# Mixed inputs made transposed by TensorE at once, with the residual turned back by VectorE

## The chip, the cores and the metric

The kernel runs on one core of a Trainium2 chip. The metric is device time in microseconds (us) for one execution; lower is better. All arithmetic is in fp32.

The engines are named as in the profile: PE is TensorE's matmuls and PEld its weight loads, DVE is VectorE, ACT is ScalarE, POOL is GpSimd, SP is SyncE, which here only issues DMAs.

## The reference

There are 64 batches of 32 tokens with 512 features. Two layers with residuals follow each other:

```python
x = x + einsum('bct,bcd->bdt', x, W[cond])     # per batch one of 16 matrices, 32x32, mixes the 32 tokens
q, k, v = x @ Wq.T, x @ Wk.T, x @ Wv.T         # 32 query heads, 8 key/value heads, 128 wide
q, k = rope(rmsnorm(q)), rope(rmsnorm(k))
kc, vc = k_cache[block_table], v_cache[block_table]      # 512 cached tokens for each batch, masked by length
probs = softmax(mask(q @ concat(kc, k).T * SCALE))
x = x + (probs @ concat(vc, v)) @ Wo.T
```

The first line is what the change is about. Its result is called x1 below. It is needed twice: transposed (features on the partitions), as the stationary or moving side of the projections, and in rows, as the residual of the second layer.

## The kernel before

**Tiling.** Four batches make a tile of 128 rows (tokens); there are NT = 16 tiles. The 8 key/value heads are worked on in two halves (hh = 0 and 1) of 4. So there are 32 steps, n = hh * 16 + t, each with one tile and one half of the heads. A step has 4 batches x 4 slots = 16 slots of about 4 us each. The inputs x1 are made in the first half alone; the second half reads what was kept in DRAM.

**What sets the order.** SP and PE run in the order in which the program issues; for the opening (all before the slots of step 0) that goes for every engine, elsewhere a scheduler places the rest. Each piece of work that isn't attention is put into a slot by `at(n, slot, ...)`; within a slot it comes in the order of these calls. A store that a piece puts into `kept` is issued on SP KEEP = 2 slots later.

**x1 of a tile, step by step.**
- `x1_a` (L383 on) loads 128 rows of x into `st.acc`. `load_cond_weights` (L288) loads the four batches' 32x32 matrices onto the diagonal of a zeroed 128x128 buffer `bds[t % 2]`, called bd; two such buffers take turns.
- `x1_c` (L404) is one matmul, with bd as weights and the 512 columns of `st.acc` moving, into PSUM (L408); DVE adds the result to `st.acc` (L409), which then holds x1 in rows.
- `x1_b` (L411) makes four 128x128 transposes of `st.acc` on PE with the identity `ident` (L416) into PSUM, and ACT copies them to `st.x1t` (L421).
- `keep_x1t` (L426) and `keep_x1` (L429) store both to DRAM: x1t_d for the second half's projections, acc_d for the residual. `reload` (L974) brings the residual back, when the step's output is to be added to it.

**What uses it.** Steps 0 to 3 are projected one by one (L470, up to `classic`). From step 4 on, two tiles make a `Pair`, whose projections use Strassen's products (in Winograd's form) of 2x2 blocks: `sums_x` (L669 to L673) makes sums of the inputs' blocks on DVE, t2, t3 and t4 (L726 to L733) sums of the weights' blocks, and seven products, "1" to "7", run on PE (L698, in PSUM tiles pa, pb, pc). The pair's x1t lie in one buffer, `early`, with room for seven blocks: two of the first tile, two of the second, and three of sums. The fourth sum, L673, has no room of its own and is written over a block of the second tile's x1t; so it waits until the store of that x1t (L426) has read it. Product 6 uses t2, which stands behind L673 on DVE.

In the first half, a pair's inputs are made in the last slots of the step before the pair's products (`input_of`): mix of the first tile in slot 11, of the second in 12, turned in 13 and 14. For the first pair that has these (n = 4) all is later: 14, 14, 15, 15. For the pair before that (n = 2) they are in slots 4 to 7 of step 2 itself.

**Beside it.** In every slot four score matmuls (L1027, 128x128 weights and 128 columns moving), the exponential on ACT (L1038) and the value matmuls (L1090) run; nv_x (L1101) are DVE's sums of the values. The keys come over SP, a half of a batch at a time in eight DMAs of 64 KB (k_t, L321), and DVE copies them to the buffers kh_x (L1018). Cached values come by indirect DMAs on POOL (L354) and are scaled by ACT (L366). Query and key rows go through L540 (a 32x32-block transposition on DVE), the DRAM buffer heads_d (L544, POOL) and SP (q_ring, L553) to their columns; in the opening and the first steps they go through PE (L527) and a copy (L612).

**The opening.** Tile 0's x1 is made while the projections' weights are still being loaded; `keep_warm` are matmuls whose results are not used. Tile 1's mix and transposes stand between attention work of tile 0.

The kernel can also run an exact version of the attention (`exact`), after a test of the denominators; with these inputs it isn't entered.

Of the kernel before, what the change touches and what calls it, by code (L numbers as in the profile page):

```python
# [12 lines left out]
F32 = mybir.dt.float32  # L13
# [47 lines left out]
def cond_resid_paged_attention_kernel(  # L61
# [118 lines left out]
    def other_half(by):  # L180
# [2 lines left out]

    x1t_d = [
        dram.tile([P, KC * P], F32, tag=f"x1t_d{t}", name=f"x1t_d{t}") for t in range(NT)
    ]
    acc_d = [dram.tile([P, HID], F32, tag=f"acc_d{t}", name=f"acc_d{t}") for t in range(NT)]
    rot_d = {
# [14 lines left out]
    def steps_of(exact, pools):  # L203
# [200 lines left out]
        def x1_c(st):  # L404
            if st.hh:
                return
            pm = ps_p.tile([P, 512], F32, tag="pp", name=f"pmix_{st.name}")
            nc.tensor.matmul(pm, bds[st.t % 2], st.acc, start=True, stop=True)  # L408
            nc.vector.tensor_tensor(st.acc, pm, st.acc, ALU.add)  # L409

        def x1_b(st):  # L411
            if st.hh:
                return
            pm = ps_p.tile([P, KC, P], F32, tag="pp", name=f"px1t_{st.name}")
            for c in range(KC):
                nc.tensor.transpose(pm[:, c, :], st.acc[:, c * P : (c + 1) * P], ident)  # L416
# [4 lines left out]
            nc.scalar.copy(st.x1t, pm)  # L421
            if st.n or exact:
                kept.append(lambda: keep_x1t(st, nc.sync))

        def keep_x1t(st, eng):
            eng.dma_start(x1t_d[st.t], st.x1t.rearrange("p c q -> p (c q)"))  # L426

        def keep_x1(st, eng=nc.sync):
            eng.dma_start(acc_d[st.t], st.acc)  # L429

        trigs = {}

# [538 lines left out]

        def reload(st):
            st.acc = work.tile([P, HID], F32, tag="acc", name=f"res_{st.name}", bufs=2)
            nc.sync.dma_start(st.acc, acc_d[st.t])  # L974

        def new_ot(st):
            st.ot = act.tile([P, QH, P], F32, tag="ot", name=f"ot_{st.name}", bufs=2)
# [273 lines left out]
        number = conditions(0, mybir.EngineType.DVE)  # L1251
        for i in range(BT):
            blk = slice(i * S, (i + 1) * S)
            nc.vector.tensor_copy(
                bds[0][blk, blk], w_all[:, bass.ds(number[i], 1), :].rearrange("p o e -> p (o e)")
            )
        x1_c(first)
        keep_warm(4)
        x1_b(first)
        keep_warm(3)  # L1260
        load_cond_weights(1)
        load_w("q", 0, 3)
        later = Batch(first, 1)
# [39 lines left out]
        for c in (0, 1):  # L1303
            batch.fill(c)
            fetch(1, c)
        v_copy(first, new)
        x1_c(second)
        batch.fill(2)
        fetch(1, 2)
# [2 lines left out]
        values(batch, 0)  # L1312
        q_a(first, 3)
        q_b(first, 2)
        x1_b(second)
        keep_x1(second, nc.gpsimd)
        head_keys(later, 0, nc.scalar)
        head_keys(later, 1, nc.scalar)
        after.load_half()
        rot_tables(second)  # L1320
        k_a(second)
        q_b(first, 3)
        scores(batch, 1)
        scores(batch, 3)
# [33 lines left out]
        def input_of(st, n, load, weights, mix, turned_at):  # L1358
            at(weights[0], weights[1], lambda: load_cond_weights(st.t))
            if load:  # L1360
                at(load[0], load[1], lambda: x1_a(st))
            at(n, mix, lambda: x1_c(st))
            at(n, turned_at, lambda: x1_b(st), lambda: kept.append(lambda: keep_x1(st)))

# [50 lines left out]
        for pair in pairs:  # L1415
            s0, s1 = pair.both
            n = s0.n - 2
            if n == 2:
                input_of(s0, 2, (1, 15), (1, 15), 4, 5)
                input_of(s1, 2, None, (2, 2), 6, 7)  # L1420
                ahead[2, 1].append(lambda st=s1: x1_a(st))
                at(2, 8, lambda: shift_w(0, 0))
                at(2, 9, lambda pair=pair: sums_x(pair))
                angles_of(2, 1, 9, 9)
                tables_of(pair, "q", 2, 8)
                tables_of(pair, "k", 3, 2)
                set_of(pair, 0, 2, {9: "t2", 10: "1", 11: "6 2 t3", 12: "5 t4", 13: "3 7", 14: "4"})
                at(3, 1, lambda: shift_w(0, 1))
                set_of(pair, 1, 3, {2: "t2", 3: "1 6 t3", 4: "2 5 t4", 5: "3", 6: "7", 7: "4"})
                at(3, 6, lambda: shift_w(0, 2))  # L1430
                set_of(
                    pair, 2, 3,
                    {8: "t2 1", 9: "2 t3", 10: "6 t4", 11: "7", 12: "4", 13: "5", 14: "3"},
                )
                spread_of(s0, 3, (12, 12, 13, 13))
            else:
                at(n, 2, lambda pair=pair: sums_x(pair, (0,)))
                at(n, 3, lambda pair=pair: sums_x(pair, (1,)))
                if pair.hh:
                    at(n - 1, 7, lambda st=s0: load_x(st))  # L1440
                    at(n - 1, 10, lambda st=s1: load_x(st))
                    tables_of(pair, "q", n - 1, 6)
                    tables_of(pair, "k", n, 7)
                else:
                    late = int(n == 4)
                    m = (n - 1, 7)
                    input_of(s0, n - 1, m, (n - 1, 6), 11 + 3 * late, 13 + 2 * late)
                    input_of(s1, n - 1, m, (n - 1, 7), 12 + 2 * late, 14 + late)
                    angles_of(s0.n // 2, n - 1, 4, 4 if late else 6)
                    if late:  # L1450
# [99 lines left out]
        for st in steps:  # L1550
            for bt in range(0 if st.n else 1, BT):
# [3 lines left out]
                for g in range(GH):  # L1555
# [27 lines left out]
                    norm_end()  # L1583
                    stores += [(st.n * BT * GH + slot + KEEP, keep) for keep in kept]
                    kept.clear()
                    if slot == 3 and st.n > 1 and st.n - 1 in alone:
                        reload(steps[st.n - 1])
                    if slot == 2 and st.n in twos:
                        reload(twos[st.n].s0)
# [131 lines left out]
```

## Time and profile before

| | |
|---|---|
| median of 3 runs | 2073.85 us (2072.66 to 2074.44) |
| the profiled execution's own time | 2073.99 us |
| its span in the trace | 2072.1 us |
| mean granted clock of TensorE | 0.997 |
| bytes moved by DMA | 413.33 MB, mean 199 GB/s |
| mix L408, a tile, on the chain | 0.86 us |
| four transposes L416, a tile, on the chain | 0.44 us |

How the profile is read: times are in us unless marked ns. A group's row has the line of the program, the engine, the operation, output<-inputs, the shape, and the count. The chain of waits that ended last is followed back from the last instruction, at each step to what released it; as a list in time it has start, duration and what. A timeline row has start, duration, engine, line, operation, and in brackets the idle time before it with what ended it. "x4" is the number of instructions in a row. "q1" in the list of queues is SP's queue: packets, MB, share of 16 DMA engines. "SPq" are DMA issues by SP. A line of waits has the waiting instruction, what ended its waits, us in total, times, longest.

### The profile page before, as it was taken

What the parts mean: (1) busy time and instruction counts of PE and PEld (TensorE: products, weight loads), DVE (VectorE), ACT (ScalarE), POOL (GpSimd) and SP (SyncE); (2) the same over time, 40 slices, a digit from 0 to 9 for tenths busy, and PEclk for the clock granted to TensorE, in tenths of its full rate; (3) what the DMA queues carried; (4) which work ended last, traced back from release to release, by engine and by line L of the source; (5) the groups of instructions that cost most, each with busy time, mean ns of one, the idle gap of its engine ahead of it and who ended that gap; (6) DMA issues with size and microseconds to landing.
All of it is one profiled execution on the core that took longest, in us unless ns stands there. A gap on an engine that the chain in (4) does not pass through costs nothing.

```text
span 2072.1 us, 45314 instructions
## 1 busy us (share of the span) xinstructions
PE 2044.2 (99%) x13460; PEld 1596.7 (77%) x13460; DVE 1629.5 (79%) x3533; ACT 958.4 (46%) x2707; POOL 1002.9 (48%) x1138
## 2 busy tenths in 40 slices
PE   8999999999999999999999999999999999999998
PEld 4767667787887878778786677878878788787897
DVE  4555687988969789697996769879797887979854
ACT  4444354444545444454434445344454445445351
POOL 4354465645636455363544445445363544536351
PEclk9999999999999999999999999999999999999999
DMA  8767557667676666787767876676767667676682
GB/s 244 198 183 223 154 153 233 184 196 217 180 219 191 210 201 189 212 265 223 217 190 208 233 207 195 196 206 180 213 182 216 185 193 210 184 211 180 191 233 75
DMA packets 410144, 413.33 MB, mean 199 GB/s; under 512 B 58944, under 2 KB 325824, under 8 KB 409888
## 3 DMA queue, kind: packets, MB, share of 16 engines
q1 hardware_dynamic: 353472, 228.55, 38.3%
q0 software_dynamic: 55680, 181.58, 28.7%
q8 instruction: 109, 1.79, 0.4%
q14 instruction: 147, 1.20, 0.2%
q10 hardware_dynamic: 736, 0.21, 0.0%
HBM read 350.09 MB, written 60.03 MB: 198 GB/s over the span
## 4 chain that ended last, share of the span: by engine, by line
PE 79%; DVE 7%; DMA 6%; SPq 3%; issue 3%; POOL 2%; ACT 1%; DVEq 0%; POOLq 0%; ACTq 0%
PE ps_x L1027 18%; PE po_x L1090 17%; PE p_x L837 13%; PE pb_x L698 8%; PE pc_x L698 6%; PE pa_x L698 5%; PE pout_x L794 3%; DMA k_t_x<-in_kt_dram 3%; SPq L321 2%; PE pnv_x L1072 2%; PE pp_q_x L470 2%; PE psn_x L1048 1%; DMA raw_x<-in_vc_dram,v_row 1%; PE pp_v_x L470 1%; DVE kh_x L1018 1%
## 5 line engine op out<-in xcount | busy, mean ns | idle before, releaser
L354 POOL DMA_INDIRECT raw_x<-in_vc_dram,v_row x512 | 550.7, 1076 | 626.7 <-ACT v_ring_x L366 513.2
L1038 ACT ACTIVATE pr_x<-ps_x 128x512 f32<-128x512 f32 x511 | 305.4, 598 | 777.5 <-PE ps_x L1027 772.4
L1090 PEld LDWEIGHTS po_x<-v_ring_x,pr_x 128*128 128x128 f32 x4088 | 523.5, 192 | 85.4 <-issue 67.3
L1027 PE MATMUL ps_x<-q_ring_x,kh_x 128*128 128x128 f32 x4088 | 547.7, 277 | 1.6 <-ACT q_ring_x L612 1.6
L1090 PE MATMUL po_x<-v_ring_x,pr_x 128*128 128x129 f32 x4088 | 544.1, 276 | 2.2 <-DVE nv_x L1101 2.2
L1027 PEld LDWEIGHTS ps_x<-q_ring_x,kh_x 128*128 128x128 f32 x4088 | 499.7, 192 | 13.9 <-issue 3.3
L366 ACT ACTIVATE v_ring_x<-raw_x,valid 128x512 f32<-128x512 f32 x512 | 342.9, 713 | 21.9 <-DMA raw_x<-in_vc_dram,v_row 21.5
L1018 DVE COPY kh_x<-k_t_x 128x512 f32<-128x512 f32 x506 | 218.6, 432 | 97.3 <-PE ps_x L1027 68.2
L544 POOL DMA_DIRECT2D heads_d<-rows_x x150 | 125.8, 839 | 278.0 <-DVE rows_x L540 211.1
L698 PE MATMUL pb_x<-t_x,early 128*128 128x512 f32 x504 | 238.4, 596 | 2.6 <-DVE t_x L726 1.2
L1101 DVE TENSOR_TENSOR nv_x<-po_x,nv_x 128x258 f32<-128x258 f32 x256 | 106.8, 417 | 101.3 <-PE po_x L1090 96.6
L837 PEld LDWEIGHTS p_x<-wo_x,ot_x 128*128 128x128 f32 x624 | 116.8, 190 | 62.1 <-issue 45.8
L488 POOL TENSOR_TENSOR rs_q_x<-ms_q_x,minus_half 128x4 f32<-128x4 f32 x128 | 158.7, 1240 | 10.7
L837 PE MATMUL p_x<-wo_x,ot_x 128*128 128x256 f32 x624 | 156.4, 380 | 0.1
L837 PE MATMUL p_x<-ts_x,ot_x 128*128 128x256 f32 x624 | 145.5, 380 | 0.0
L698 PEld LDWEIGHTS pb_x<-t_x,early 128*128 128x128 f32 x504 | 86.2, 191 | 65.4 <-issue 60.6
L837 PEld LDWEIGHTS p_x<-ts_x,ot_x 128*128 128x128 f32 x624 | 115.6, 191 | 24.2 <-issue 8.4
L1104 DVE TENSOR_TENSOR nv_x<-nv_x,rden 128x256 f32<-128x256 f32 x256 | 109.5, 428 | 8.7
L479 ACT ACTIVATE sq_q_x<-u_x 128x128 f32<-128x128 f32 x224 | 66.3, 298 | 93.9 <-DVE u_x L714 93.9
L698 PE MATMUL pc_x<-wq_x,early 128*128 128x512 f32 x224 | 105.4, 593 | 0.0
L698 PE MATMUL pa_x<-wq_x,early 128*128 128x512 f32 x224 | 105.4, 593 | 0.0
L514 DVE TENSOR_TENSOR rope_q_x<-rope_q_x,rs_q_x 128x512 f32<-128x512 f32 x120 | 82.2, 685 | 19.7 <-POOL rs_q_x L488 19.3
(207 smaller groups left out, 2629.6 us busy)
## 6 DMA issues: line engine op xcount, KB each, us to landing
k_t_x<-in_kt_dram SPq DMA_DIRECT2D x2048, 64.0 KB
heads_d<-rows_x POOLq DMA_DIRECT2D x150, 256.0 KB
q_ring_x<-heads_d SPq DMA_DIRECT2D x464, 80.0 KB
raw_x<-in_vc_dram,v_row POOLq DMA_INDIRECT x512
wo_x<-in_wo_dram SPq DMA_DIRECT2D x32, 256.0 KB
res_x<-acc_d SPq DMA_DIRECT2D x31, 256.0 KB
wq_x<-in_wq_dram SPq DMA_DIRECT2D x8, 512.0 KB
early<-x1t_d SPq DMA_DIRECT2D x16, 256.0 KB
```

Source lines behind the costliest of these rows:

```text
L354: nc.gpsimd.indirect_dma_start(out=raw.rearrange("p g d -> p (g d)"), out_offset=None, in_=vc, in_offset=bass.IndirectOffsetOnAxis(ap=v_ro ...
L366: nc.scalar.activation(v_ring[:, c, :, 0:D], raw, AF.Copy, scale=valid[:, b, c : c + 1])
L488: nc.gpsimd.tensor_tensor(rs, ms, minus_half, ALU.pow)
L544: nc.gpsimd.dma_start(heads_d[st.n][:, :, i, :].rearrange("k p c -> p k c"), part)
L698: nc.tensor.matmul(bank, pair.x[:, i, c, :], by[:, c * 512 : (c + 1) * 512], start=start and c == 0, stop=c == 1, skip_group_check=not start,)
L837: nc.tensor.matmul(to, left[:, i, :], right(i), start=start and i == 0, stop=i == QH // 2 - 1, skip_group_check=True,)
L1018: nc.vector.tensor_copy(to, src)
L1027: nc.tensor.matmul(ps[:, c, i, :], ba.k[j][:, i, c, :], queries(ba, g + i), start=True, stop=True,)
L1038: nc.scalar.activation(pr, ps, AF.Exp, scale=SCALE)
L1090: nc.tensor.matmul(ba.po[g][:, i, :], ba.pr[j][:, c, i, :], ba.v_t[:, 2 * half + c, g + i, :], start=(half == 0 and c == 0 and i == 0), st ...
L1101: nc.vector.tensor_tensor(t, ba.po[g], t, ALU.add)
L1104: nc.vector.tensor_tensor(t[:, :, 0:D], t[:, :, 0:D], rd.unsqueeze(2).to_broadcast([P, 2, D]), ALU.mult,)
```

## The change

- `x1_c` no longer mixes rows. The rows of x are the weights, in four chunks of 128 features, and bd moves, with the identity added: out = chunk^T (bd + I), which is x1 of this chunk, transposed. ACT copies it to `st.x1t` in this slot.
- `with_own` adds the identity to bd on DVE, one slot before the mix. For tile 0 it is added in the four copies that build bd.
- `x1_b` no longer uses PE: DVE turns x1t back with its transposition of 32x32 blocks. The blocks then don't lie in rows of 512: partition s of group k holds, for each chunk c and each batch b, 32 features of token s of b.
- `keep_x1` undoes that on the way to DRAM, into a new buffer x1_d: four DMAs for a tile, of 32 partitions x 16 runs of 128 bytes each. `reload` in the first half reads it by four DMAs, one for a batch (32 x 4 runs of 512 bytes).
- Step 0's residual is now reloaded too.
- In the opening, tile 0 is turned back and kept behind `v_copy(first)`; tile 1 is turned back and kept behind `k_a(second)`.
- In pairs from n = 4 on, the mix is in slots 13 and 14 (n = 4: 14, 15) and the turning in 14 and 15 (15, 15). The new matmuls then stand in PE's order where the transposes stood. In SP's order the four stores of the first tile's x1 come between the two tiles' x1t stores.

```diff
         def x1_c(st):
             if st.hh:
                 return
-            pm = ps_p.tile([P, 512], F32, tag="pp", name=f"pmix_{st.name}")
-            nc.tensor.matmul(pm, bds[st.t % 2], st.acc, start=True, stop=True)
-            nc.vector.tensor_tensor(st.acc, pm, st.acc, ALU.add)
+            pm = ps_p.tile([P, KC, P], F32, tag="pp", name=f"pmix_{st.name}")
+            bd = bds[st.t % 2]
...
+            for c in range(KC):
+                nc.tensor.matmul(
+                    pm[:, c, :],
+                    st.acc[:, c * P : (c + 1) * P],
+                    bd,
+                    start=c == 0,
+                    stop=c == KC - 1,
+                    skip_group_check=True,
+                )
+            x1_copy(st, pm)
...
         def x1_b(st):
             if st.hh:
                 return
-            pm = ps_p.tile([P, KC, P], F32, tag="pp", name=f"px1t_{st.name}")
-            for c in range(KC):
-                nc.tensor.transpose(pm[:, c, :], st.acc[:, c * P : (c + 1) * P], ident)
...
-            nc.scalar.copy(st.x1t, pm)
...
+            nc.vector.transpose(
+                st.acc.rearrange("p (j d) -> p j d", d=S),
+                st.x1t.rearrange("p c (b s) -> p (c b) s", s=S),
+            )
+
+        def with_own(t):
+
+            bd = bds[t % 2]
+            nc.vector.tensor_tensor(bd, bd, ident, ALU.add)
...
         def keep_x1(st, eng=nc.sync):
-            eng.dma_start(acc_d[st.t], st.acc)
+            for k in range(4):
+                eng.dma_start(
+                    x1_d[st.t][:, :, :, k * S : (k + 1) * S].rearrange("s c b d -> s (c b) d"),
+                    st.acc[k * S : (k + 1) * S].rearrange("s (j d) -> s j d", d=S),
+                )
...
         def reload(st):
             st.acc = work.tile([P, HID], F32, tag="acc", name=f"res_{st.name}", bufs=2)
-            nc.sync.dma_start(st.acc, acc_d[st.t])
+            if st.hh:
+                nc.sync.dma_start(st.acc, acc_d[st.t])
+                return
+            for b in range(BT):
+                nc.sync.dma_start(
+                    st.acc[b * S : (b + 1) * S].rearrange("s (c d) -> s c d", c=KC),
+                    x1_d[st.t][:, :, b, :],
+                )
...
         x1_c(first)
-        keep_warm(4)
-        x1_b(first)
-        keep_warm(3)
+        keep_warm(6)
...
         v_copy(first, new)
+        x1_b(first)
+        keep_x1(first, nc.gpsimd)
+        with_own(1)
         x1_c(second)
...
         q_b(first, 2)
-        x1_b(second)
-        keep_x1(second, nc.gpsimd)
...
         k_a(second)
+        x1_b(second)
+        keep_x1(second, nc.gpsimd)
...
+            at(n, mix - 1, lambda: with_own(st.t))
             at(n, mix, lambda: x1_c(st))
...
-                    input_of(s0, n - 1, m, (n - 1, 6), 11 + 3 * late, 13 + 2 * late)
-                    input_of(s1, n - 1, m, (n - 1, 7), 12 + 2 * late, 14 + late)
+                    input_of(s0, n - 1, m, (n - 1, 6), 13 + late, 14 + late)
+                    input_of(s1, n - 1, m, (n - 1, 7), 14 + late, 15)
...
-                    if slot == 3 and st.n > 1 and st.n - 1 in alone:
+                    if slot == 3 and st.n and st.n - 1 in alone:
                         reload(steps[st.n - 1])
```

More of the change, by code (lines that the diff above doesn't have):

```diff
@@ L185, in cond_resid_paged_attention_kernel @@
         dram.tile([P, KC * P], F32, tag=f"x1t_d{t}", name=f"x1t_d{t}") for t in range(NT)
+    ]
+    x1_d = [
+        dram.tile([S, KC, BT, P], F32, tag=f"x1_d{t}", name=f"x1_d{t}") for t in range(NT)
     ]
@@ L406, in x1_c, with x1_copy @@
                 return
-            pm = ps_p.tile([P, 512], F32, tag="pp", name=f"pmix_{st.name}")
[L408 to L412, printed above, removed]
+            pm = ps_p.tile([P, KC, P], F32, tag="pp", name=f"pmix_{st.name}")
+            bd = bds[st.t % 2]
+            if exact:
+                flat = pm.rearrange("p c q -> p (c q)")
+                nc.tensor.matmul(flat, bd, st.acc, start=True, stop=True)
+                nc.vector.tensor_tensor(st.acc, flat, st.acc, ALU.add)
                 return
-            pm = ps_p.tile([P, KC, P], F32, tag="pp", name=f"px1t_{st.name}")
             for c in range(KC):
-                nc.tensor.transpose(pm[:, c, :], st.acc[:, c * P : (c + 1) * P], ident)
+                nc.tensor.matmul(
[7 more added lines that the diff above has]
+            x1_copy(st, pm)
+        def x1_copy(st, pm):
             if st.pair is None:
@@ L423, in x1_b @@
                 kept.append(lambda: keep_x1t(st, nc.sync))
+        def x1_b(st):
+            if st.hh:
+                return
+            if exact:
+                pm = ps_p.tile([P, KC, P], F32, tag="pp", name=f"px1t_{st.name}")
+                for c in range(KC):
+                    nc.tensor.transpose(pm[:, c, :], st.acc[:, c * P : (c + 1) * P], ident)
+                x1_copy(st, pm)
+                return
+            nc.vector.transpose(
[5 more added lines that the diff above has]
+            nc.vector.tensor_tensor(bd, bd, ident, ALU.add)
         def keep_x1t(st, eng):
@@ L973, in reload @@
             st.acc = work.tile([P, HID], F32, tag="acc", name=f"res_{st.name}", bufs=2)
-            nc.sync.dma_start(st.acc, acc_d[st.t])
+            if st.hh:
+                nc.sync.dma_start(st.acc, acc_d[st.t])
+                return
+            for b in range(BT):
[3 more added lines that the diff above has]
+                )
         def new_ot(st):
@@ L1253, in steps_of @@
             blk = slice(i * S, (i + 1) * S)
-            nc.vector.tensor_copy(
-                bds[0][blk, blk], w_all[:, bass.ds(number[i], 1), :].rearrange("p o e -> p (o e)")
+            nc.vector.tensor_tensor(
+                bds[0][blk, blk],
+                w_all[:, bass.ds(number[i], 1), :].rearrange("p o e -> p (o e)"),
+                ident[0:S, 0:S],
+                ALU.add,
             )
         x1_c(first)
-        keep_warm(4)
-        x1_b(first)
-        keep_warm(3)
+        keep_warm(6)
         load_cond_weights(1)
```

## The prediction

> **What bounds the kernel now.** I read the page's busy line first, then the shares of the chain that ended last.
>
> ```profile
> span 2072.1 us, 45314 instructions
> ...
> PE 2044.2 (99%) x13460; PEld 1596.7 (77%) x13460; DVE 1629.5 (79%) x3533; ACT 958.4 (46%) x2707; POOL 1002.9 (48%) x1138
> ...
> PE 79%; DVE 7%; DMA 6%; SPq 3%; issue 3%; POOL 2%; ACT 1%; DVEq 0%; POOLq 0%; ACTq 0%
> ...
> q1 hardware_dynamic: 353472, 228.55, 38.3%
> ```
>
> TensorE is busy 99% of the span. In its timeline I looked for stretches over 0.3 us in which it does nothing: behind the opening (from 76 us on) they come to some 15 us in all. So a matmul that goes there is worth its own time, and a wait of any other engine costs only once it is longer than what PE still has to do. The chain of waits in order of time shows the price of the groups, here around tile 2 (start, us, group):
>
> ```profile
> 102.36 0.86 PE pmix_x L408 x2
> 103.22 0.89 PE po_x L1090 x8
> 104.12 0.89 PE ps_x L1027 x8
> 105.01 0.44 PE px1t_x L416 x4
> ```
>
> A plain fp32 matmul has two records: the mix (512 columns) costs 2 x 0.43 us, the four 128-column score matmuls 8 x 0.11 = 0.89 us. A transpose has one: 4 x 0.11 = 0.44 us.
>
> **Part 1, TensorE.** Per tile the mix and the transposes go (0.86 + 0.44 = 1.30 us) and four plain matmuls come: 128x128 weights, 128 columns moving, the form of L1027, 0.89 us. That is 0.41 us less for a tile, if nothing else is late.
> - Tiles 2, 3 and 6 to 15: the new group stands where the transposes stood. Its new partner is the identity's addition, a slot earlier on DVE (128x128, some 0.3 us by the L141 row of that shape). I placed it in the timeline: it ends 2 to 9 us ahead of the matmuls. 12 x 0.41 = **-4.9 us**.
> - Tiles 4 and 5: there the mix is only a few us behind DVE.
>
> ```profile
> 191.13 1.02 PE L408 MATMUL pmix_x<-read_x,bd 128*128 128x512 f32 x2
> 191.20 0.71 DVE L540 STREAM_TRANSPOSE rows_x<-rope_k_x 128x512 f32<-128x512 f32 x1
> ...
> 198.12 0.63 PE L416 MATMUL px1t_x<-ident,read_x 128*128 128x128 f32 x4 [0.75 <-DVE read_x L409]
> ```
>
> The addition is queued behind that L540, so it ends near 192.2, and PE would stand about 1.1 us; behind PE waits the whole of slots 4 and 5. Tile 5 the same: mix was at 203.81, the addition behind L540 (203.38 to 204.09) and the new 0.71 us transposition, so near 205.0, again 1.1 us. Against it stand the 0.75 us wait above, which goes with the add L409, and 2 x 0.41. Sum 2.2 - 0.8 - 0.8: **+0.6 us**. If DVE is earlier than I think, -1.6.
> - Tiles 0 and 1: tile 0's mix and transposition lie under the opening's weight loads.
>
> ```profile
> 24.75 7.89 DMA wv_x<-in_wv_dram
> ...
> 32.78 6.30 PE pp_v_x L470 x8
> ...
> 49.00 0.50 ACT x1t_x L421
> ...
> 49.54 3.71 PE pp_k_x L470 x8
> ```
>
> Nothing before 32.78 gains: worth 0. For tile 1, PE stands 1.6 us before pp_k for the copy L421; now the copy can run from 44 us, and pp_k comes about 2.1 us earlier. But the transposes of the fourth query group, behind it, need DVE's rows L514 (their last ends near 52.9), and their copy L612 stood behind ACT's squares until 54.55, now some 54.2. So **-0.9 us** (between 0 and -2.1).
>
> Sum of part 1: -4.9 + 0.6 - 0.9 = **-5.2 us**.
>
> **Part 2, VectorE.** The add L409 (0.69 us) goes; a stream transposition of the same size (0.71 by L540) and the addition of the identity (0.3) come: 0.3 us more for a tile, 5 us in all. In the last slots before a pair's products DVE stands for nv_x and kh_x (0.4 to 1.5 us at a time near 456 to 466): that hides it. Without that cover it would be up to 5 us on kh_x. I take 0.
>
> ```profile
> L409 DVE TENSOR_TENSOR read_x<-pmix_x,read_x x12: 652/688/692, 197.3 to 826.4; 128x512 f32<-128x512 f32 x12
> L540 DVE STREAM_TRANSPOSE rows_x<-rope_q_x x120: 711/711/714, 130.0 to 1918.8; 128x512 f32<-128x512 f32 x120
> L429 SPq DMA_DIRECT2D acc_d<-read_x x12: 410/436/1024, 204.6 to 848.9; - x12
> ```
>
> **Part 3, SyncE's queue.** Where one DMA kept x1 there are four, and four where one brought it back. An issue takes 0.43 us (L429 above). A pair of tiles has 6 more to keep (two tiles) and 6 more to reload, so 2 x 2.6 us, ahead of k_t issues (eight of 0.33 us a half) and ring reads. From a half's last k_t issue to the first DVE copy that uses it I measured 5.2 to 10 us in the stretches concerned; its landing takes some 2.3. So 2.6 us more are covered everywhere, by 0.3 us at the tightest (5.2 us); it is tight but not late, if the transfers themselves aren't longer. I take 0, up to 1.5 for each of the five pairs otherwise. On POOL the first two tiles add six issues of some 0.7 us at 50 to 59 us; POOL is idle from 56 to 65, and the gathers before that have a margin I put inside the bounds of tile 1.
>
> **Part 4, the wait that becomes later.** The x1t buffer of a pair's second tile is overwritten by DVE's sum L673, so that sum waits until x1t has been read out:
>
> ```profile
> DVE early L673 <- DMA x1t_d<-early: 8.0, 4, 3.3
> ```
>
> and the third pair shows what hangs on it:
>
> ```profile
> 598.00 0.43 SPq L429 DMA_DIRECT2D acc_d<-read_x  x1
> ...
> 601.13 0.42 DVE L673 TENSOR_TENSOR early<-early 128x256 f32<-128x256 f32 x1 [3.29 <-DMA x1t_d<-early]
> 601.48 1.22 DVE L726 TENSOR_TENSOR t_x<-wq_x 128x1024 f32<-128x1024 f32 x1
> ...
> 603.98 1.88 PE L698 MATMUL pb_x<-t_x,early 128*128 128x512 f32 x4
> ```
>
> The sum runs, then the weights' sum L726 (1.22 us), then PE's pb. From L726's end at 602.70 to pb is a margin of 1.3 us; for the five pairs I measured 1.5, 3.3, 1.3, 4.2 and 4.7 us. In the changed order the first tile's four x1 DMAs go out directly ahead of the second's x1t: 1.05 us later for the first pair, 1.75 for the rest, plus B, the time that 2,048 packets of 128 bytes take on DMA engines which are 75 to 100% busy in these stretches (the gathers of V fill them). The trace holds no 128-byte write to DRAM. Its packet records say 9 ns for 4 bytes, 12 ns for 128 bytes (reads of the condition weights, 2,432 of them), 28 ns for 512 bytes, 104 ns for 2 KB. So B is 2048 x 12 / 16 = 1.5 us. The row store that it replaces took 128 x 104 / 16 = 0.8 us, and I can't see how much of that lay ahead of x1t before: I take half, so 0.4 less, 1.1. The other end is 28 ns, B = 3.6 - 0.4 = 3.2. I take 12 ns, the row of the same size. By pair, lateness less margin: 1.05 + 1.1 - 1.5 = 0.65; 1.75 + 1.1 - 3.3 below 0; 1.75 + 1.1 - 1.3 = 1.55; 0; 0. That is 2.2 us, with 0.2 for tight k halves **+2.4 us**. With 20 ns (B = 2.1) it is 1.65 + 0.55 + 2.55 + 0 + 0, about 4.8; with 28 ns 2.75 + 1.65 + 3.65 + 0.75 + 0.25 = 9, and up to 5 x 1.5 more from part 3.
>
> One page of the Trainium skill speaks against this layout. "DMA: Bandwidth & Descriptors", Specifications, names 512 bytes as the least transfer for full rate, and has writes below it done as a read, a change and a write back. If that doubled the 12 ns, the stall would be near 7 us instead of 2.4; no row here shows such a write. Another page, "TensorE: Matmul & The Clock Gate", gives a transpose as four times faster than a plain fp32 matmul on trn2; the chain above shows two (0.44 against 0.89 us), and by the page the new group would cost 1.75 us, a loss of 0.45 for a tile instead of a gain of 0.41. The measured rows decide, since L1027 is the same shape.
>
> **Sum.** -5.2 + 2.4 = -2.8 us on the profiled execution's 2073.99 us (span 2072.1 and 1.9 around it), which is within 0.14 of the median 2073.85: **2071.2 us**. A difference under 0.2% (4.15 us) is about what a measurement of this kernel cannot tell from no change.
>
> **Rivals.**
> - No stall (chance 0.22). The margins hold and tiles 4 and 5 don't wait: -4.9 - 1.6 - 0.9, and up to 1.2 more from tile 1: -6 to -8.6, **2067**. For it: pb's margin is over 3 us in three of five pairs. Against: the 3.3 us wait already in the profile.
> - Slow small writes (0.24). 128-byte writes cost 28 ns or more: x1t's read-out is late in all five pairs, and PE stands before pb: 9 us, and 4 more with the k halves half-way to their bound: 13 - 5.2 = +7.8, **2081.8**. It decides from some 20 ns a packet, where gain and loss meet. For it: 32,768 packets take the place of 2,048, at engines that are already full there; 28 ns on all of them is 57 us of the 16 engines' time against 13. Against: 12 ns for reads of this size.
> - The gain is just eaten (0.15): 16 to 20 ns a packet (3.4 to 4.8 us of stall), and k halves late by up to 0.7 us in each pair: -1.8 to +3, **2074.5**.
> - The change doesn't do what it says (0.04): a group with inputs as weights costs more than L1027 because weights have to be loaded four times for a tile instead of once. PE's weight loads are 192 ns each and run beside, so 0.2 us a tile at most: -2.8 + 3.2, **2074.4**.
>
> The forecast case has 0.35, with -1.5 to -5 us as its own range, 2069 to 2072.5; a third of it lies past 0.2%. Faster: 0.22 + 0.13 = 0.35. Slower: nearly all of 0.24 = 0.24. The same: the rest, 0.41. The range takes in no stall without its extremes and slow writes to their middle: 2066 to 2082, with some 0.08 left out on each side.
>
> **What would show it.** In the changed profile: a group of four matmuls with eight records of 0.11 us for each tile, no transposes (step 1 right; 1.3 us or more makes it wrong). PE standing about 1 us for DVE near 192 and 205 us (tiles 4, 5). No wait of PE before pp_k near 49 us. L673's waits for x1t_d grown from 8.0 us by 2 to 3 us in each of five pairs, and gaps of PE before pb only in the first and third. The packet records of 128-byte writes: about 12 ns is my case, 20 or more the slow one. PE gaps in all five pairs, or kh_x late behind k_t, make the forecast wrong upward; a span short by 6 us or more, downward.

## The result

The changed kernel takes 2105.65 us (median of 6 runs, 2097.50 to 2110.78). The kernel before, on the same chip, takes 2074.14 us (6 runs, 2069.38 to 2075.44). The ratio is 1.0151, with a 95% interval of 1.0137 to 1.0166: 31 us **slower** (28 to 34). The forecast was 2071.2, with a range of 2066 to 2082. The profiled execution took 2109.22 us.

### The profile after

The page of the changed kernel: its span, busy times, the shares of the chain that ended last, and SP's queue.

```profile
span 2107.3 us, 45516 instructions
...
PE 2048.8 (97%) x13490; PEld 1598.3 (76%) x13490; DVE 1635.3 (78%) x3548; ACT 954.2 (45%) x2707; POOL 1010.5 (48%) x1145
...
PE 71%; SPq 10%; DMA 6%; DVE 6%; issue 4%; ACT 1%; POOL 1%; DVEq 0%; ACTq 0%; POOLq 0%
...
q1 hardware_dynamic: 388080, 228.82, 38.6%
```

PE's busy time hardly differs (the slower passes told of below are in it), but the chain runs 10% through SP's queue, where it was 3%. SP moves the same bytes (228.82 MB against 228.55); the 34,600 added packets are next to nothing in the engines' share, 38.6% against 38.3%. So the time is neither PE's work nor the engines' load: something waits for SP.

To find where, I set each slot's length (start of one score group L1071 to the next) beside the same slot of the kernel before. Most slots agree within 0.05 us. What differs by more, in us (slots 5 and 9 are summed over the five pairs that have their products in steps 4, 6, 8, 10 and 12):

| place | changed kernel | what it is |
|---|---|---|
| opening, up to tile 2's mix | -2.3 | tiles 0 and 1 |
| step 2, slots 4 to 7 | +1.4 | tiles 4 and 5: 1.17, -1.38, 2.04, -0.44 |
| inputs of the other twelve tiles | -4.8 | -0.41 a tile; in the later pairs -0.86 in slots 11 and 12 (the mix), +0.45 in 13 and 14 |
| slot 5 of the five steps | +15.5 | 3.9, 1.3, 1.3, 4.9, 4.0: the wait for x1t's read-out |
| slot 9 of the five steps | +24.7 | 5.4, 5.4, 5.5, 6.4, 2.0: a half of the keys comes late |

Two stops a pair, some 40 us in all, are the loss. What the table leaves out is under 1 us in sum: single slots of steps 3, 12, 13 and 17 shift by 1 to 2 us, both ways. In the changed kernel's timeline of step 8, this is DVE:

```profile
617.86 0.42 DVE L710 TENSOR_TENSOR early<-early 128x256 f32<-128x256 f32 x1 [5.76 <-DMA x1t_d<-early]
618.21 1.22 DVE L763 TENSOR_TENSOR t_x<-wq_x 128x1024 f32<-128x1024 f32 x1
...
637.79 0.43 DVE L1062 COPY kh_x<-k_t_x 128x512 f32<-128x512 f32 x1 [4.58 <-DMA k_t_x<-in_kt_dram]
...
640.13 0.68 DVE L751 TENSOR_TENSOR u_x<-pb_x,u_x 128x512 f32<-128x512 f32 x1
```

and this PE, in the same stretch:

```profile
619.48 1.98 PE L735 MATMUL pb_x<-t_x,early 128*128 128x512 f32 x4 [1.07 <-DVE t_x L763]
...
632.81 1.88 PE L735 MATMUL pb_x<-t_x,early 128*128 128x512 f32 x4
...
640.87 3.67 PE L735 MATMUL pb_x<-t_x,early 128*128 128x512 f32 x4 [3.53 <-DVE u_x L751]
```

The first stop is the one of part 4: L710 (before: L673) waits 5.76 us for x1t_d, then L763, then PE. The second is new. In the kernel before, the same copy of keys and the same product stood in step 8 without a wait:

```profile
617.46 0.43 DVE L1018 COPY kh_x<-k_t_x 128x512 f32<-128x512 f32 x1
```

```profile
621.45 1.88 PE L698 MATMUL pb_x<-t_x,early 128*128 128x512 f32 x4
```

Now DVE stands 4.58 us in its queue for kh_x, L751 stands behind it, and PE waits 3.53 us for L751. It also costs more than its wait: after it the same four matmuls take 3.67 us instead of 1.88. The windows view (columns: window, length, busy time of each engine with counts, PE's granted clock, DMA share, GB/s) shows the clock in the changed kernel's stretch:

```profile
604.00:628.00 24.00, 22.93 (x162) 18.02 (x161) 14.23 (x33) 11.42 (x30) 8.17 (x9) 1.00 0.78 218
627.00:652.00 25.00, 21.47 (x116) 15.73 (x115) 19.43 (x40) 10.50 (x36) 10.84 (x12) 0.93 0.63 183
```

The stretch with the 1.07 us wait is granted 1.00, the one with the 3.53 us wait 0.93. The Trainium skill ("TensorE: Matmul & The Clock Gate", Part 1) says that PE falls to half its clock after an idle window of about 3.4 us. The traces here agree only in part. Of the ten stops of the changed kernel, seven are followed by matmuls wholly or partly at half pace, and two of these come after waits of only 1.97 and 2.02 us. In the run with the small runs on the kernel before, told of below, a wait of 3.24 us is followed by full pace. Here are the first from the changed kernel and the last from that run:

```profile
350.70 3.63 PE L735 MATMUL pb_x<-t_x,early 128*128 128x512 f32 x4 [1.97 <-DVE t_x L763]
```

```profile
636.72 1.98 PE L702 MATMUL pb_x<-t_x,early 128*128 128x512 f32 x4 [3.24 <-DVE u_x L718]
```

So the length of the wait alone doesn't decide here, and what does was not found.

What SP does then, in the changed kernel's timeline and in that of the kernel before:

```profile
611.27 2.69 SPq L463 DMA_DIRECT2D x_d<-read_x  x4
614.07 0.56 SPq L459 DMA_DIRECT2D x1t_d<-early  x1
614.73 2.99 SPq L463 DMA_DIRECT2D x_d<-read_x  x4
617.96 4.05 SPq L324 DMA_DIRECT2D k_t_x<-in_kt_dram  x8
622.03 5.21 SPq L1015 DMA_DIRECT2D res_x<-x_d  x8
627.42 1.87 SPq L590 DMA_DIRECT2D q_ring_x<-heads_d  x4
630.59 5.56 SPq L324 DMA_DIRECT2D k_t_x<-in_kt_dram  x8
```

```profile
603.02 0.90 SPq L974 DMA_DIRECT2D res_x<-acc_d  x2
604.10 1.71 SPq L553 DMA_DIRECT2D q_ring_x<-heads_d  x4
607.10 4.00 SPq L321 DMA_DIRECT2D k_t_x<-in_kt_dram  x8
```

In the changed kernel SP goes from one issue to the next nearly without a pause; the 1.3 us ahead of 630.59 is work of SP's too, the reading of page numbers (L304). The half of the keys whose copy is late is issued from 630.59 to 636.2; the copy wants it at 633.2 (637.79 less 4.58). Eight reload issues took 5.21 us where two took 0.90, and an x1 store takes not 0.43 us but:

```profile
L463 SPq DMA_DIRECT2D x_d<-read_x x48: 562/627/1068, 206.1 to 885.7; - x48
```

```profile
L1015 SPq DMA_DIRECT2D res_x<-x_d x64: 442/597/1237, 116.9 to 1145.6; - x64
```

(The three figures are the least, the median and the longest, in ns.)

### The profile page after: what moved, and what is told of

It is laid out like the page before. It is cut to its first block, busy times and chain, and to the rows that moved or that the text cites. A ratio compares the mean times of both kernels' runs of the same rounds, so it can differ in the third digit from the quotient of the medians.

```text
span 2107.3 us, 45516 instructions
## 1 busy us (share of the span) xinstructions
PE 2048.8 (97%) x13490; PEld 1598.3 (76%) x13490; DVE 1635.3 (78%) x3548; ACT 954.2 (45%) x2707; POOL 1010.5 (48%) x1145
## 3 DMA queue, kind: packets, MB, share of 16 engines
q1 hardware_dynamic: 388080, 228.82, 38.6%
## 4 chain that ended last, share of the span: by engine, by line
PE 71%; SPq 10%; DMA 6%; DVE 6%; issue 4%; ACT 1%; POOL 1%; DVEq 0%; ACTq 0%; POOLq 0%
PE po_x L1134 16%; PE ps_x L1071 16%; PE p_x L874 12%; PE pb_x L735 8%; SPq L324 6%; PE pa_x L735 5%; PE pc_x L735 5%; PE pout_x L831 3%; DMA k_t_x<-in_kt_dram 2%; PE pnv_x L1116 2%; DMA q_ring_x<-heads_d 2%; SPq L590 1%; PE pp_q_x L507 1%; PE psn_x L1092 1%; DMA wq_x<-in_wq_dram 1%
## 5 line engine op out<-in xcount | busy, mean ns | idle before, releaser
L357 POOL DMA_INDIRECT raw_x<-in_vc_dram,v_row x512 | 559.6, 1093 | 623.2 <-ACT v_ring_x L369 513.2
L1071 PE MATMUL ps_x<-q_ring_x,kh_x 128*128 128x128 f32 x4088 | 547.6, 277 | 2.0 <-ACT q_ring_x L649 1.2
L1071 PEld LDWEIGHTS ps_x<-q_ring_x,kh_x 128*128 128x128 f32 x4088 | 499.3, 192 | 14.3 <-issue 3.8
L735 PE MATMUL pb_x<-t_x,early 128*128 128x512 f32 x504 | 249.5, 619 | 29.7 <-DVE u_x L751 18.6
L525 POOL TENSOR_TENSOR rs_q_x<-ms_q_x,minus_half 128x4 f32<-128x4 f32 x128 | 157.9, 1234 | 10.7
L551 DVE TENSOR_TENSOR rope_q_x<-rope_q_x,rs_q_x 128x512 f32<-128x512 f32 x120 | 82.2, 685 | 16.5 <-POOL rs_q_x L525 16.1
```

What stands on the lines that cost most here:

```text
L357: nc.gpsimd.indirect_dma_start(out=raw.rearrange("p g d -> p (g d)"), out_offset=None, in_=vc, in_offset=bass.IndirectOffsetOnAxis(ap=v_ro ...
L525: nc.gpsimd.tensor_tensor(rs, ms, minus_half, ALU.pow)
L735: nc.tensor.matmul(bank, pair.x[:, i, c, :], by[:, c * 512 : (c + 1) * 512], start=start and c == 0, stop=c == 1, skip_group_check=not start,)
L1071: nc.tensor.matmul(ps[:, c, i, :], ba.k[j][:, i, c, :], queries(ba, g + i), start=True, stop=True,)
```

## The experiments

**The theory** at the outset: the DMAs of the new layout make the loss. They hold up x1t's read-out (first stop) and they hold SP, so that a half of the keys is late (second stop). **The rivals**: DVE's new work does it; the small runs do it by loading the engines; all comes from the late x1t. Times below are against the runs of the kernel before on the same chip: 2076.62 us for the first four, 2072.16 for the next, 2072.37 for the last.

### Whole rows, one DMA each way

```diff
-            for k in range(4):
-                eng.dma_start(x1_d..., st.acc...)
+            eng.dma_start(acc_d[st.t], st.acc)
...
-            if st.hh:
-                nc.sync.dma_start(st.acc, acc_d[st.t])
-                return
-            for b in range(BT):
-                nc.sync.dma_start(st.acc..., x1_d...)
+            nc.sync.dma_start(st.acc, acc_d[st.t])
```

> The changed kernel, but x1 is kept by one DMA of whole 2 KB rows and brought back by one. It leaves out the undoing of the block order: the residual of the first half is added in the wrong order of its elements. Theory (the loss of 31 us lies in the small-run DMAs: they hold up the read-out of x1t, they hold SP, and PE's waits cost its clock as well): all of the five stops of about 9 us each go, 44 us in all, and 2066 to 2071 us remain. Rival (the transposition back and the identity's addition put DVE's order out, and the stops before pb are DVE's own): 2090 us or more.

Measured: 2073.84 us, ratio 0.9986 (0.9972 to 1.0000), so -2.9 us (-5.8 to 0). Neither stop is there, though everything else of the change is. So the DMAs are the whole loss, and DVE's work is none of it. The gain that is left is small: 2073.84 lies above the 2066 to 2071 that I expected, on a chip where the kernel before took 2076.62.

### x1t's store first

```diff
-                kept.append(lambda: keep_x1t(st, nc.sync))
+                kept.append((0, lambda: keep_x1t(st, nc.sync)))
...
-            at(n, turned_at, lambda: x1_b(st), lambda: kept.append(lambda: keep_x1(st)))
+            at(n, turned_at, lambda: x1_b(st), lambda: kept.append((1, lambda: keep_x1(st))))
...
-                    stores += [(st.n * BT * GH + slot + KEEP, keep) for keep in kept]
+                    stores += [(st.n * BT * GH + slot + KEEP, keep) for _, keep in sorted(kept, key=lambda one: one[0])]
```

> The changed kernel, but where stores come due in one slot, the x1t stores are issued ahead of the x1 stores; nothing else. Theory (two stops for a pair, of two causes: L710 waits for x1t's read-out, some 14 us in all; SP's issues push a half of the keys late, some 24 us in all): only the first cause goes, L710's waits fall from 32 us to under 15, and the time falls by 8 to 14 us, to 2092 to 2098. Rival (both stops come from the late x1t): 2075 or less. Rival (x1t is late because of the engines' load, not of the order): within 3 us of 2105.

Measured: 2110.34 us, +34 (+30 to +38). My expectation failed. The slots below are those of the profiled execution, the fastest of the run's five (2099.4 us; the others took 2110 to 2112). The stop in slot 5 did go (0.0 in all five, L710's waits fell from 32.4 to 11.7 us), but 12.1 us came back in slot 7 (2.5, 1.5, 1.6, 4.2, 2.3). There PE now waits for L888, the sum with the reloaded residual (6.9 us in all): SP's lateness found the next thing that hangs on it. Slot 9 stayed at 18.8 us. So a better order of the same issues didn't help.

### The DMAs alone, on the kernel before

```diff
-            eng.dma_start(acc_d[st.t], st.acc)
+            for k in range(4):
+                eng.dma_start(
+                    acc_d[st.t].rearrange("p (c q) -> p c q", c=KC)[:, :, k * S : (k + 1) * S],
+                    st.acc.rearrange("p (c q) -> p c q", c=KC)[:, :, k * S : (k + 1) * S],
+                )
...
-            nc.sync.dma_start(st.acc, acc_d[st.t])
+            for c in range(1 if st.hh else KC):
+                cols = slice(0, HID) if st.hh else slice(c * P, (c + 1) * P)
+                nc.sync.dma_start(st.acc[:, cols], acc_d[st.t][:, cols])
```

> The kernel before, but x1 is kept in four DMAs of 128-byte runs (each a stripe of 32 of every 128 columns, 512 runs) and brought back in the first half in four DMAs of 512-byte runs; the DRAM layout stays that of rows. TensorE, VectorE and the slots stay as before. Theory (the DMAs alone make the loss): +30 to +45 us, 2104 to 2119, with the same two stops in the five pairs. Rival (they need the change's order of work on DVE and its late slots to hurt): under +10 us.

Measured: 2099.73 us, +22 (+17 to +27). Less than I expected, but with PE's and DVE's work untouched most of the loss is there: 21.2 us in slot 9, and 1.0 in slot 5.

### Four DMAs of whole rows

```diff
+            for k in range(4):
+                eng.dma_start(acc_d[st.t][k * S : (k + 1) * S], st.acc[k * S : (k + 1) * S])
...
+            for b in range(1 if st.hh else BT):
+                rows_of = slice(0, P) if st.hh else slice(b * S, (b + 1) * S)
+                nc.sync.dma_start(st.acc[rows_of], acc_d[st.t][rows_of])
```

> The changed kernel with four DMAs for the store and four for the reload, but each of 32 whole rows of 2 KB. It leaves out the undoing of the block order, as the run with one DMA does. It tells the number of issues from the size of the runs. Theory (both count: issues 0.43 us each instead of 0.62 to 1.07, and no packets of 128 bytes): the first stop goes, the second stays in part, 2072 to 2085. Rival (only the number of issues counts): 2095 or more. Rival (only the small runs count): 2066 to 2071, like the run with one DMA.

Measured: 2101.86 us, +25 (+18 to +31): the rival that I had set at 2095 or more. Against the run with one DMA each way, the bytes and the data packets of 2 KB are the same, and what differs is the number of DMAs: 28 us. An issue of this form takes SP 0.42 us, hardly less than one of 128 rows (0.43). Slot 9 holds 16.1 us of it, slot 5 8.9. So the loss doesn't need the small runs. What they may add (31 against 25 us) is within the intervals. The packet records agree: in the changed kernel, with 28,672 more packets of 128 bytes, nearly all writes, the mean of that size is 13.4 ns, where the reads alone took 12.2 in the kernel before. The read, change and write back of which the Trainium skill speaks ("DMA: Bandwidth & Descriptors", Specifications) did not show as a doubled time.

### Stores alone, reloads alone, both

```diff
-            eng.dma_start(acc_d[st.t], st.acc)
+            for b in range(BT):
+                eng.dma_start(acc_d[st.t][b * S : (b + 1) * S], st.acc[b * S : (b + 1) * S])
```

> The kernel before, with x1 stored in four DMAs of 32 whole rows instead of one of 128; reload as before. Theory (SP has no idle time from a pair's x1t stores to its third slot, so each added issue pushes the next halves of the keys back by 0.45 us; stores and reloads add up in one place): six issues more for a pair, 2.7 us; part of it lies under the slack of the halves, so +3 to +12 us over the five pairs, less than half of the run with both. Rival (the delay of x1t's read-out is the cause): nearly the whole loss, +15 to +25. Rival (small runs are the cause): 0.

```diff
-            nc.sync.dma_start(st.acc, acc_d[st.t])
+            for b in range(1 if st.hh else BT):
+                part = slice(0, P) if st.hh else slice(b * S, (b + 1) * S)
+                nc.sync.dma_start(st.acc[part], acc_d[st.t][part])
```

> The kernel before, with the first half's residuals brought back in four DMAs of 32 whole rows instead of one of 128; stores as before. Theory (SP's issues, as in the run with four stores): six issues more for a pair at the third slot, straight ahead of the half of the keys that came late in the changed kernel: +5 to +15 us. Rival (x1t's read-out): 0, as the reloads come behind it.

Measured: 2073.68 us each, +1.0 (-1.0 to +2.9) for the stores and +2.1 (-0.4 to +4.8) for the reloads: under both of my expectations. Six issues more cost nothing that can be told. Then both edits in one kernel:

> The kernel before with both of the edits that made nothing alone: four whole-row DMAs for each x1 store and four for each first-half reload. Theory (the added issues add up in one stretch, and only the sum goes past the slack of the halves of the keys): +15 to +26 us, where the two alone gave 0 and +2. Rival (stores and reloads add up only as they did alone): under +4.

Measured: 2087.39 us, +12 (+8 to +17); stops in slot 9 of 5.0, 3.3, 2.8, 0.7 and 4.8 us. Two edits that cost next to nothing each make 12 together: there is a point up to which added issues are free. This is DVE, then SP, in step 8 of that kernel:

```profile
627.40 0.43 DVE L1021 COPY kh_x<-k_t_x 128x512 f32<-128x512 f32 x1 [3.61 <-DMA q_ring_x<-heads_d]
```

```profile
618.93 4.04 SPq L321 DMA_DIRECT2D k_t_x<-in_kt_dram  x8
```

The last of the half's eight DMAs is issued by 622.97, and the copy can run only at 627.40, 4.4 us later; in step 8 of the changed kernel it was 1.6 us (636.15 to 637.79), and over all runs the copies that had to wait came 1.5 to 5.6 us behind the last issue. (The profile puts the wait down to q_ring, whose issue comes behind the half; kh_x reads k_t.) POOL issued two gathers of values at 620.77 and 622.05, in the middle of it. A late half may then fall in with the next gathers and land later still; that is read from the trace and wasn't tried by itself.

### Issues with next to no bytes

```diff
             eng.dma_start(acc_d[st.t], st.acc)
+            if st.n:
+                for k in range(3):
+                    eng.dma_start(tiny_d[st.t][k : k + 1], ident[k : k + 1])
...
             nc.sync.dma_start(st.acc, acc_d[st.t])
+            for k in range(0 if st.hh else 3):
+                nc.sync.dma_start(tiny_d[st.t][3 + k : 4 + k], ident[k : k + 1])
```

> The kernel before, with three DMAs of 512 bytes each (the identity's rows to a scratch buffer that nothing reads) on SP behind each x1 store and behind each first-half reload: 12 more issues for a pair at the changed kernel's places, and next to no bytes. Theory (SP's issue time is what costs, 12 x 0.45 us in one full stretch): the stop in slot 9 of the five pairs comes, +12 to +26 us. Rival (the DMAs' transfers cost, split into more and shorter ones): within 3 us of the kernel before.

Measured: 2075.79 us (2071.58 to 2090.43), +3.3 (+0.2 to +6.6): nearer to the rival. The same number of issues as in the run with both, and a quarter of the loss. This run doesn't part the two rivals, since a tiny DMA has next to no bytes and also takes SP less time (7.5 us a pair against 9.8). The profiled execution is the slowest of ten, 2090.43 us, but only 1.4 us of its loss lies in slot 9; the rest is spread over steps 10, 13, 18, 30 and 31, and why was not settled.

### Stores later, and an earlier addition

The pairs' x1 stores come due eleven slots later, where SP has pauses (1.0 to 6.5 us each in the kernel before, from 632 us on):

```diff
+LATER = 11
...
-lambda: kept.append(lambda: keep_x1(st))
+lambda: kept.append((LATER if n > 2 else 0, lambda: keep_x1(st)))
...
-                    stores += [(st.n * BT * GH + slot + KEEP, keep) for keep in kept]
+                    stores += [(st.n * BT * GH + slot + KEEP + more, keep) for more, keep in kept]
+                    stores.sort(key=lambda one: one[0])
```

> The changed kernel, but the pairs' x1 stores are issued eleven slots later, where SP has idle time; reloads stay at the third slot. Theory (SP is full in the first slots): the stores' part goes, the reloads' part stays, 2080 to 2095, and L710's waits fall to those of the kernel before or under (8 us, at most 12). Rival (the engines are held by small packets wherever they go): 2100 or more.

Measured: 2070.35 us, ratio 0.9989 (0.9974 to 1.0005). The same DMAs, with the same small runs, and the whole loss is gone; L711's (L710's) waits are 8.3 us, as before the change. I had expected the reloads to keep a part, but alone they are under the free amount. It is not shown to be faster than the kernel before.

```diff
-            at(n, mix - 1, lambda: with_own(st.t))
+            at(n, mix - (2 if n == 2 else 1), lambda: with_own(st.t))
```

> The changed kernel with late x1 stores, and the identity added to bd two slots ahead of the mix instead of one in the first pair (tiles 4 and 5). Theory: in tiles 4 and 5 PE's waits of 1.1 and 1.9 us for the addition go, 2.4 us in all, 2066 to 2069. Rival (the addition stands elsewhere in DVE's way): within 1 us of the run with late stores alone.

Measured: 2073.53 us (12 runs), ratio 1.0003 (0.9988 to 1.0018). The step went half as meant: tile 4's slot fell from +1.17 to +0.03 us, tile 5's stayed at +1.64. There the addition was done at 197.70 us, but PE's mix at 203.40 waited until ACT's squares (sq_q, L517) ended at 203.35. In the changed kernel the squares end at 202.50, the addition at 202.85 and the mix starts at 202.95, so the addition cost tile 5 at most 0.4 us. Why PE waits for these squares was not settled. The microsecond doesn't show in the time.

### Other queues

The same DMAs on ACT's queue, then the stores alone on POOL's:

```diff
-        def keep_x1(st, eng=nc.sync):
+        def keep_x1(st, eng=nc.scalar):
...
-                nc.sync.dma_start(
+                nc.scalar.dma_start(
                     st.acc[b * S : (b + 1) * S].rearrange("s (c d) -> s c d", c=KC),
```

> The changed kernel, but the slots' x1 stores and all first-half reloads and the other reloads' four-part form are issued by ACT on its own queue instead of SP; sizes and runs are the changed ones. Theory (what costs is SP's issue time): all five losses go, and what is left is the change's gain on PE, 2066 to 2074. Rival (the DMAs themselves, their small runs or the load of the DMA engines): 2090 or more. Rival (ACT waits in its queue for DVE's transposition or for the stores' buffers and its exponentials come late): 2076 to 2090, with PE waiting for pr_x.

Measured: 2154.46 us, +83 (+78 to +88), far past every case that I had named. It is also not the same loss: slots 5 and 9 have no stop in any of the five pairs, and the time goes in slots 2 to 4 (43 us in slot 4 alone). ACT's and PE's waits in this kernel, and ACT's issues in step 8:

```profile
ACT pr_x L1082 <- DMA res_x<-x_d: 49.1, 7, 10.7
```

```profile
PE pa_x L735 <- ACT z_x L776: 37.3, 6, 9.5
```

```profile
634.30 8.14 ACTq L1015 DMA_DIRECT2D res_x<-x_d  x8
```

An exponential stood up to 10.7 us behind a reload in ACT's queue. The Trainium skill ("Perfetto Trace Analysis", DMA Optimizations) names balancing DMAs over the engines that can issue them as something that may help where issuing is the bound; here ACT's own stream is what PE waits for, and the measurement decides.

```diff
-lambda: kept.append(lambda: keep_x1(st)))
+lambda: kept.append(lambda: keep_x1(st, nc.gpsimd)))
```

> The changed kernel, but the slots' x1 stores are issued by POOL instead of SP, in the changed slots. Theory (SP's sum): with six issues fewer on SP than in the kernel before for its stores, no stop is left, if POOL has time: 2066 to 2075. Rival (POOL then holds up its gathers of cached values, 0.8 us an issue, 6.4 us a pair): 2080 to 2110, with ACT waiting for raw_x.

Measured: 2079.04 us, +8.5 (+4.8 to +12). ACT's waits for raw_x grew, from 21.5 us before to 31.7, and the first stop came back in one pair:

```profile
732.69 0.42 DVE L710 TENSOR_TENSOR early<-early 128x256 f32<-128x256 f32 x1 [7.22 <-DMA x1t_d<-early]
```

In between the two cases, then. Yet slot 9 tells more than the time: its stop falls from 24.7 to 1.7 us. In step 8 POOL issues the two tiles' stores at 589.32 and 594.76 us, two slots behind the turning as before, with the same small runs, the same packets and the same reloads on SP. What has changed is the queue that issues the stores. So the second stop follows SP's issuing and not the stores' transfers. Of the loss that is left, 4.5 us are the first stop (4.2 of it in one pair); the rest may come from the later gathers, which wasn't tried.

### All runs side by side

For each pair I took SP's time for the stores and reloads between the first tile's x1t store and the late half of the keys, and where PE stood (in slots, counted by score groups) at that half's first issue. Medians over the five pairs; the position is given for the third pair (the run on ACT's queue is left out):

| run | issues | SP, us a pair | PE's slot | slot 9, us in all | against before, us |
|---|---|---|---|---|---|
| kernel before | 6 | 2.9 | 134 | | |
| one DMA, whole rows | 6 | 2.8 | 134 | 0 | -2.9 |
| four stores on the kernel before | 12 | 6.5 | 135 | 0 | +1.0 |
| four reloads on the kernel before | 12 | 6.6 | 134 | 0 | +2.1 |
| changed, stores late | 10 | 6.2 | 135 | 0.6 | -2.3 |
| changed, stores on POOL | 10 | 6.2 | 135 | 1.7 | +8.5 |
| tiny DMAs on the kernel before | 18 | 7.5 | 135 | 1.4 | +3.3 |
| four DMAs of whole rows | 18 | 8.8 | 136 | 16 | +25 |
| both on the kernel before | 18 | 9.8 | 136 | 17 | +12 |
| small runs on the kernel before | 18 | 11.7 | 136 | 21 | +22 |
| x1t's store first | 18 | 12.5 | 136 | 19 | +34 |
| changed kernel | 18 | 12.3 | 136 | 25 | +31 |

Slot 9's stop goes with SP's time for the issues. Up to some 6.6 us a pair it is next to nothing, and from 8.8 on the half goes out two slots late and the stop is there; the tiny DMAs, at 7.5, are the only run between. How far past it a run falls goes with SP's time only roughly (8.8 cost 25 us, 9.8 cost 12), since the stop in slot 5 comes on top in some. The run with the stores on POOL parts SP's time from their transfers: the same small runs move in the same slots, and slot 9 has 1.7 us.

## Why the prediction was wrong

- **Part 1, TensorE: right in kind.** The group of four plain matmuls has eight records and costs what I took; on the changed kernel's chain around tile 2:

```profile
100.04 0.89 PE pmix_x L418 x8
```

  Twelve tiles give -0.41 us each, as forecast. Tiles 4 and 5 cost +1.4 instead of +0.6: PE's waits there were 0.90 and 1.77 us, and the second was mostly one for ACT's squares, which the sum didn't have. Tiles 0 and 1 gave -2.3 instead of -0.9 in the changed kernel, but between -2.6 and +1.1 in the other runs with the change, so a gain there is not shown. The idle stretches of PE that the text puts at some 15 us come to 10.2 us in the trace. The sum of part 1 was -5.2 us; the run with one DMA each way measures -2.9 (-5.8 to 0).
- **Part 2, VectorE: right.** With the new work on DVE and the old DMAs neither stop is left.
- **Part 3, SyncE's queue: this step failed.** It said "So 2.6 us more are covered everywhere, by 0.3 us at the tightest". Three things were wrong with it. I took the stores' 2.6 us and the reloads' 2.6 us as two places, each with its own slack; SP has no pause between them, so they add up in front of one half of the keys. In the kernel before, there was no gap over 0.15 us from 332 to 348 us, and in all five pairs none over 0.35 us from the first x1t store to the reloads, the reading of page numbers counted as work. I took 0.43 us an issue from the row of 128 rows; the new forms take 0.63 and 0.60. And I took 2.3 us for a half's landing, where the copies that waited came 1.5 to 5.6 us behind its last issue. So 9.4 us came in one place (12.3 against 2.9), where I had 2.6 in each of two, and the late half alone cost 24.7 us in slot 9 where I had 0. The first of the three is the one that failed the step: each 2.6 alone is covered, as the text said (+1.0 for the stores, +2.1 for the reloads), and at 0.42 us an issue, the price that I took, four DMAs of whole rows still stop slot 9 for 16 us. I had looked at the slack of each half and never at SP's own idle time.
- **Part 4: the mechanism was right, its size was not.** L673's waits grew from 8.0 to 32.4 us, and 15.5 us reach PE, where I had 2.4. The packets took 13.4 ns against my 12, so B was not what failed: x1t was issued later than I thought (four stores at 0.7 us ahead of it, and SP already late), and landed behind them. In step 8, x1t's store is issued at 614.07, L710 runs at 617.86, and PE gets product 6 at 619.48, 1.07 us after it wanted it.
- **What a stop costs.** I priced a stop at its wait. The 3.53 us wait made the next four matmuls 1.8 us longer as well, and seven of the ten stops were followed by slower matmuls.
- **The rivals.** The slow one had the right place and the right sign, +7.8 us, but the wrong cause (28 ns a packet) and a quarter of the size.

The places, the wait of L673 and a late kh_x, were in the text; the range ended below the measured time because each was priced alone.

## What to carry to other kernels

A queue that issues without a pause has no slack of its own, however much each of its transfers has: look at its idle time in the stretch first, and add up everything that the change puts into that stretch. Cutting one DMA into four cost the issuing engine nearly four times as much here (0.42 us each against 0.43), with the same bytes and data packets. Up to the slack this is free and past it steep: two edits that cost next to nothing alone cost 12 us together here, and moving the issues to where the queue pauses got all of the loss back.

## What was not expected of the hardware

- An issue on SP isn't one price: 0.33 us for k_t, 0.43 for a store of 128 rows of 2 KB, 0.42 for one of 32 rows of 2 KB, 0.63 for 32 partitions with 16 runs of 128 bytes, 0.60 for 32 partitions with 4 runs of 512 bytes.
- Writes of 128 bytes to DRAM took 13.4 ns a packet (with 2,432 reads among them), about what reads of that size take (12.2).
- What a stop costs beyond its wait did not go by the length of the wait: four matmuls of 1.88 us took 3.67 after 3.53 us and 3.63 after 1.97 us, and 1.98 after 3.24 us.
- The slots of step 13, near 908 us, are up to 5 us longer in most of the runs with the change, and also in the run with the tiny DMAs. PE waits there for ACT, and ACT for gathered values (2.4 to 3.4 us); why the gathers are late was not settled.
